# A transformer block with spline-coded feed-forward weights: a third key tile turned by VectorE, x loaded turned, shorter weight sums

## The chip, the core and the metric

The kernel runs on one core of a Trainium2 chip. The metric is the device time of one execution in microseconds: 546.9 us is the median of three runs before the change (546.57 to 549.12). The engines are called PE (TensorE: matrix products and transposes through the identity matrix, with PEld as its loading of weights), DVE or VectorE, ACT or ScalarE, POOL or GpSimd, and SP, whose queue issues nearly all transfers here. Each engine takes its instructions in the order in which they were written; they wait for each other through semaphores.

## The reference

x has 4 batches of 512 tokens with 512 features. The block computes a layer norm without weights and adds two branches that both read its result:

```python
x = x + attention(xn) + ffn(xn)            # xn = (x - mean) / sqrt(var + 1e-5)
# attention: 16 heads of 32, causal
scores = q k^T / sqrt(32) + slope[h] * (key - 511)      # then the causal mask
out = (softmax(scores) @ v) @ Wo + bo
# ffn: each weight matrix (2048 x 512 or 512 x 2048) is a Catmull-Rom
# spline through 8134 control points, read row by row
inter = silu(xn @ gate_w.T) * (xn @ up_w.T)
y = inter @ down_w.T
```

A weight row is a sum of a few control points, each times a known coefficient that depends only on the position. All is in float32.

## The kernel before, in words

**Two stages.** The attention stage takes the four batches one after the other and prepares the feed-forward stage's tables beside it; the feed-forward stage then runs by written plans (line 1273, carried out by `carry_out`). The attention stage ends in the profile at 387.8 us, where the first gate product (line 1135) starts.

**Units.** The attention's work is cut into 64 units, `units` at line 850: batch b, group hg of four heads, tile i of 128 queries. Unit number n is 16 b + 4 hg + i; four units with the same b and hg are called a group here. Unit i looks at the keys of tiles 0 to i. The loop at line 1074 writes one step per unit, and in step n:

- `normalize(units[n-1])`: VectorE's reciprocal of the sums (line 907), then four scalings of p by GpSimd (909);
- `scores(u)`: PE's products for four heads (865; the step i = 0 also makes those of i = 1), then for each head one VectorE instruction that adds the distances and gives the row's minimum, "minima" below (878). The four PSUM banks of the scores are the same in each unit, so the next products wait for these;
- `exponentials(u)`: ScalarE's exp with the minimum as bias and the sum as second result (894);
- `turn(old, c)` for unit n-3: p, with keys along the free axis, must have keys on the partitions for the product with v. Key tiles c = 0 and 2 go through PE, four transposes to a `pT` copy by ScalarE (922, 923);
- `swap(n-2)`: key tiles 1 and 3 go through VectorE instead, which transposes 32x32 blocks (937); four transfers per unit then move the blocks to their partitions (`moved`, 945). For this the keys of the odd tiles are stored in another order (814 to 822), and `dists` holds the distances in that order (589 to 612). `SLOTS` lists the (query tile, key tile) pairs;
- at the end of a group's last step, `values` of the group before (966);
- `items[n]`, `small[n]` and `early[n]`: lists filled from line 988 on with what else belongs to this step: projections q and k of the next group, values of the next batch, the output projection of the batch before, statistics and norms of the next batch.

**Norm and turn of x.** For the next batch, `stat_steps` computes mean and root, `norm` writes xn with tokens on the partitions (767), and `turn_it` turns it through PE, four transposes and a ScalarE copy per token tile (782, 783), into `xnT`. Tiles 0 to 3 are normalized at units 7 to 10 of a batch and turned at 8 to 11.

**The tables of the feed-forward stage.** `row_weight_steps` (616) makes the reduced gate and up weights: eight terms, each a product of 128x1024 (646) and, but for the first, an addition (649), for two halves. `down_steps` (664) makes those of down: 14 terms of 512 or 640 columns (690, 693), five for each of two pieces and four for the third. Each takes coefficients and points that SP loads to the spare space of `feat`. `some_weights` (1068) places them, twice in each step, by a budget of estimated costs. `stretch_moments` (503) multiplies xnT by a basis (510), copies three PSUM banks out and sends them to DRAM; the buffers `out` are two, so the third copy waits for the first's transfer (525, 528). `copy_rows` (543) lets GpSimd issue the copies that gather a batch's table.

Of the kernel before, what the change touches and what calls it, by code (L numbers as in the profile page):

```python
# [12 lines left out]
F32 = mybir.dt.float32  # L13
# [5 lines left out]
P = 128  # L19
# [6 lines left out]
NG = 4  # L26
# [4 lines left out]
SLOTS = [(1, 1), (2, 1), (3, 1), (3, 3)]  # L31
# [17 lines left out]
NCV = 5  # L49
NX = 9 + 4  # L50

COPIES = (1, 1, 4, 1)
NW, NW4 = 11, 4
NST = NW4 + 1

DOWN_STEPS = [("v", lo, hi, c) for lo, hi in ((0, 5), (5, 9)) for c in range(NCV)]
DOWN_STEPS += [("m", 0, NB, c) for c in range(4)]

# [276 lines left out]

def own_points(parts, points):


    values = parts[:, :, :, :9].transpose(0, 4, 3, 1, 2)
    values = values.reshape(P, 9, 2, P // 2, NCD)  # L340
    moments = parts[:, :, :, 9:].transpose(3, 4, 0, 1, 2)
    moments = moments.reshape(P, NB, 2, P // 2, NCD)
    strip = np.broadcast_to(points[:, None, None], (NB, Q32, 9, P, NCD)).reshape(values.shape)
    group = np.broadcast_to(points[None], (P, NB, P, NCD)).reshape(moments.shape)
    own = {}
    for kind, a, number, n in (("v", values, strip, NCV), ("m", moments, group, 4)):
        hit = (a != 0.0).any(axis=3)
        first = np.where(hit.any(axis=3), hit.argmax(axis=3), 0)
        first = np.minimum(first, NCD - n)[:, :, :, None, None] + np.arange(n)
        first = np.broadcast_to(first, (*a.shape[:4], n))  # L350
        few = np.take_along_axis(a, first, axis=4)
        assert np.count_nonzero(few) == np.count_nonzero(a)
        shape = (*a.shape[:2], P, n)
        own[kind] = few.reshape(shape), np.take_along_axis(number, first, axis=4).reshape(shape)
    steps = [[a[:, lo:hi, :, c].reshape(-1) for a in own[k]] for k, lo, hi, c in DOWN_STEPS]
    return *(np.concatenate(a) for a in zip(*steps)),
# [20 lines left out]
_coef = _coef.reshape(NB, NB, P, NCG, 2, Q32).transpose(3, 1, 5, 0, 4, 2)  # L377
COEF = single(_coef.reshape(NCG, P, NB, 2, P))
# [20 lines left out]
def block_kernel(  # L399
    ctx: ExitStack,  # L400
    tc: tile.TileContext,
    xT: bass.AP,
    cols: bass.AP,
# [28 lines left out]
    feat = {0: keep.tile([P, NB, 2, S], F32, name="feat")}  # L432
    table = [dram.tile([P, NB, 2, S], F32, name=f"table{b}") for b in range(B)]
# [10 lines left out]
    edge = [keep.tile([P, S], F32, name=f"edge{k}") for k in range(2)]  # L444
    lone = [keep.tile([P, S], F32, name=f"lone{k}") for k in range(2)]
    basist = keep.tile([P, NRT, ND], F32, name="basist")
# [20 lines left out]
    dists = [wp.tile([P, S], F32, name=f"dist{k}") for k in range(2)]  # L467
# [84 lines left out]
    with ExitStack() as att:  # L552
# [19 lines left out]
        for k in range(2):  # L572
            nc.gpsimd.memset(lone[k], 0.0)
            nc.gpsimd.memset(edge[k], 0.0)
# [9 lines left out]
        nc.sync.dma_start(out=basist, in_=basis)  # L584
# [4 lines left out]
        for k, dist in enumerate(dists):  # L589
            for t in range(NB):  # L590
                part = dist[:, t * P : (t + 1) * P]
                shape, steps = part, [[1, P]]
                if t % 2 == k:
                    shape = part.rearrange("p (r y) -> p r y", y=Q32)
# [4 lines left out]
                    base=1 - S + t * P,  # L599
# [3 lines left out]
                if t == NB - 1:  # L603
# [12 lines left out]
        def row_weight_steps(first_down):  # L616
            size = NB * 2 * P
            shaped = lambda a: a.rearrange("p (q x n) -> p q x n", q=NB, x=2)
            spare = [
                feat[0].rearrange("p c h s -> p (c h s)")[:, k * size : (k + 1) * size]  # L620
                for k in range(4)
            ]
            temps = [wd[:, :size], wd[:, size : 2 * size]]
            tabs, points = {}, {}

            def load(c):
                def go():
# [735 lines left out]
```

## Time and profile before, and how to read it

| what | value |
|---|---|
| median of three runs | 546.9 us |
| the profiled execution's own time | 543.63 us |
| its span, first to last instruction | 541.4 us |
| attention stage's end (first L1135) | 387.8 us |
| PE turns of p, L922 | 384, 56.5 us busy |
| PE turns of x, L782 | 64, 9.5 us busy |
| DVE block transposes, L937 | 64, 43.4 us busy |
| ScalarE copies behind the turns, L923 and L783 | 96 and 16, 54.8 and 9.2 us busy |
| row weights, L646 and L649 | 16 and 14, 1.21 and 1.26 us each |
| down weights, L690 and L693 | 14 and 11, 0.64 to 0.86 and 0.64 to 1.20 us each |

A row such as "L922 PE MATMUL mm<-ident,p 128*128 128x128 f32 x384" names the line, the engine, the operation, what it writes and reads, its shape and its count. A float32 product appears as two records on PE. "DVE inv L907 <- ACT p L894" in the list of waits says that the first waited for the second. Matmul records overlap, since their ends are modelled: the time that PE spends on one is read from the next one's start.

### The profile page before, as it was taken

To read this page: it belongs to the slowest core of one execution; us is meant where nothing else is said; L and a number is where in the kernel's file an instruction comes from. 1 tells how busy PE (TensorE), PEld (TensorE's weight loads), DVE (VectorE), ACT (ScalarE), POOL (GpSimd) and SP (SyncE) were. 2 spreads that over 40 slices of the span, in tenths; PEclk is the share of its full clock that TensorE was granted. 3 is DMA by queue.
4 is the path that set the end of the run, shared out by engine and by line. 5 is a ranking of instruction groups with operands and counts; after the bars stand their busy time and mean duration, and the time that the engine had idled before them with its cause. 6 is when DMAs were issued, how large, how long until landed. Compare 5 with 4: busy or idle time off the path is not lost.

```text
span 541.4 us, 12182 instructions
## 1 busy us (share of the span) xinstructions
PE 530.3 (98%) x4268; PEld 268.0 (50%) x4268; DVE 352.8 (65%) x990; ACT 296.0 (55%) x798; POOL 243.8 (45%) x436
## 2 busy tenths in 40 slices
PE   7999999999999999999999999989999999999997
PEld 6645545444445544444554454545334555747552
DVE  6169978888677877667676456563135584865836
ACT  2466875665466665646757588883313433624222
POOL 3045635574266565446656567671017232332310
PEclk9999999999999999999999999979999999999999
DMA  8933487575545785745743325464656565665344
GB/s 317 321 122 70 114 213 215 160 194 155 161 144 147 243 276 166 214 142 146 215 123 89 92 67 148 137 188 118 174 165 197 184 221 197 199 203 181 119 164 166
DMA packets 63805, 92.98 MB, mean 172 GB/s; under 512 B 10528, under 2 KB 35104, under 8 KB 63232
## 3 DMA queue, kind: packets, MB, share of 16 engines
q1 hardware_dynamic: 59136, 83.79, 51.5%
q0 software_dynamic: 4608, 8.40, 5.3%
q8 instruction: 34, 0.56, 0.4%
q14 instruction: 27, 0.22, 0.1%
HBM read 50.74 MB, written 23.68 MB: 137 GB/s over the span
## 4 chain that ended last, share of the span: by engine, by line
PE 84%; DVE 5%; DMA 5%; ACT 3%; SPq 2%; issue 1%; DVEq 0%; ACTq 0%
PE mm L798 17%; PE g L1135 9%; PE mm L837 9%; PE s L865 7%; PE mm L922 7%; PE mm L482 6%; PE o L1236 6%; PE c L966 5%; PE o L1182 4%; PE o L1253 3%; PE o L482 3%; ACT p L894 2%; DVE p L878 2%; PE s L482 2%; PE mm L510 2%; PE o L1135 2%
## 5 line engine op out<-in xcount | busy, mean ns | idle before, releaser
L909 POOL TENSOR_SCALAR p<-p,inv 128x128 f32<-128x128 f32 (+3 forms) x256 | 147.5, 589 | 172.1 <-DVE inv L907 122.1
L894 ACT ACTIVATE p<-p,low 128x128 f32<-128x128 f32 (+3 forms) x256 | 141.3, 555 | 48.9 <-DVE low L878 48.3
L878 DVE CUSTOM_DVE_ANT_0 p<-s,dist 128x128 f32<-128x128 f32 (+3 forms) x256 | 108.8, 481 | 21.8 <-PE s L865 21.5
L1158 POOL COPY made<-inner 128x512 f32<-128x512 f32 x64 | 38.9, 637 | 104.2 <-DVE inner L1157 81.5
L923 ACT COPY pT<-mm 128x512 f32<-128x512 f32 x96 | 54.8, 577 | 40.3 <-PE mm L922 40.0
L1135 PE MATMUL g<-feat,wT 32*64 32x512 f32 x864 | 65.3, 592 | 0.0
L1150 ACT ACTIVATE act<-g 128x512 f32<-128x512 f32 x64 | 33.0, 602 | 57.0 <-PE g L1135 56.7
L865 PE MATMUL s<-kT,qT 32*128 32x512 f32 (+3 forms) x512 | 57.4, 479 | 2.2 <-DVE low L878 2.0
L798 PE MATMUL mm<-xnT,wk 128*128 128x512 f32 (+1 forms) x136 | 59.3, 579 | 0.2 <-ACT xnT L783 0.2
L837 PE MATMUL mm<-wv,xnT 128*128 128x512 f32 x128 | 58.1, 596 | 1.1 <-ACT xnT L783 1.1
L798 PE MATMUL mm<-xnT,wq 128*128 128x512 f32 (+1 forms) x136 | 57.8, 567 | 0.0
L922 PE MATMUL mm<-ident,p 128*128 128x128 f32 x384 | 56.5, 283 | 0.4 <-ACT pT L923 0.3
L922 PEld LDWEIGHTS mm<-ident,p 128*128 128x128 f32 x384 | 42.5, 142 | 25.6 <-issue 17.1
L894 ACT ACTIVATION_READ_ACCUMULATOR p<-p,low 128x1 f32 x256 | 48.8, 191 | 0.0
L937 DVE STREAM_TRANSPOSE blocks<-p 128x512 f32<-128x512 f32 x64 | 43.4, 696 | 0.0
L1157 DVE TENSOR_TENSOR inner<-g,act 128x512 f32<-128x512 f32 x44 | 27.3, 683 | 21.7 <-PE g L1135 10.7
L1135 PEld LDWEIGHTS g<-feat,wT 32*64 32x64 f32 x864 | 30.6, 131 | 21.3 <-issue 10.6
L865 PEld LDWEIGHTS s<-kT,qT 32*128 32x128 f32 x512 | 24.5, 186 | 32.8 <-issue 16.2
L798 PEld LDWEIGHTS mm<-xnT,wk 128*128 128x128 f32 x136 | 24.5, 189 | 25.1 <-issue 21.5
L546 POOL DMA_DIRECT2D table<-samples x64 | 36.9, 583 | 0.0
L1236 PE MATMUL o<-inner,dRM 32*64 32x512 f32 x512 | 36.6, 588 | 0.0
L798 PEld LDWEIGHTS mm<-xnT,wq 128*128 128x128 f32 x136 | 24.7, 190 | 22.4 <-issue 21.7
(105 smaller groups left out, 656.3 us busy)
## 6 DMA issues: line engine op xcount, KB each, us to landing
moved<-blocks SPq DMA_DIRECT2D x128, 64.0 KB, 2.1
moved<-blocks SPq DMA_DIRECT2D x64, 128.0 KB, 3.0
feat<-table SPq DMA_DIRECT2D x16, 512.0 KB, 4.3
inner<-made SPq DMA_DIRECT2D x32, 256.0 KB, 3.5
table<-samples POOLq DMA_DIRECT2D x64, 88.0 KB, 3.0
xp<-in_xp_dram SPq DMA_DIRECT2D x16, 256.0 KB, 5.1
feat<-in_coef_dram SPq DMA_DIRECT2D x8, 512.0 KB, 8.8
feat<-in_rowpts_dram SPq DMA_DIRECT2D x32, 128.0 KB, 5.1
```

The costliest lines, as they stand in the source:

```text
L482: nc.tensor.matmul(ps, lhsT=wsb["o"][:, c, r * P : (r + 1) * P], rhs=ctxT[b][:, c, :], start=(c == 0), stop=(c == NB - 1),)
L798: nc.tensor.matmul(ps[0][:, tokens], lhsT=wsb[name][:, c, hg * P : (hg + 1) * P], rhs=xnT[b][:, c, tokens], start=(c == 0), stop=(c == NB ...
L837: nc.tensor.matmul(ps[0], lhsT=xnT[b][:, c, t * P : (t + 1) * P], rhs=wsb["v"][:, c, :], start=(c == 0), stop=(c == NB - 1),)
L865: nc.tensor.matmul(banks[b, hg][j][:, at : at + (k + 1) * P], lhsT=qk[b, hg, "q"][rows, k * P : (k + 1) * P], rhs=qk[b, hg, "k"][rows, : ( ...
L878: nc.vector.tensor_tensor_reduce(out=p[:, j, :nk], in0=ps[j], in1=dists[i % 2][:, S - nk :], scale=-SLOPES[hg * NG + j], scalar=BIG, op0=A ...
L894: nc.scalar.activation(p[:, j, :nk], p[:, j, :nk], AF.Exp, bias=low[:, j : j + 1], scale=-1.0, accum_out=total[:, j : j + 1],)
L909: nc.gpsimd.tensor_scalar(p[:, j, :nk], p[:, j, :nk], inv[:, j : j + 1], 1.0, ALU.mult, ALU.mult)
L922: nc.tensor.transpose(ps[:, j, :], p[:, j, c * P : (c + 1) * P], ident)
L923: nc.scalar.copy(pT[b, hg, c][:, :, (i - c) * P : (i - c + 1) * P], ps)
L937: nc.vector.transpose(own[:, :, k].rearrange("p r j k -> p j r k"), soft[u][0][:, :, c * P : (c + 1) * P].rearrange("p j (r k) -> p j r k" ...
L1135: nc.tensor.matmul(ps[k][cols, :], lhsT=wT[rows, q, 2 * w + part, cols], rhs=feat[b][rows, q, part, :], start=(part == 0), stop=(part == 1),)
L1236: nc.tensor.matmul(sums[b][r][cols, :], lhsT=dR[rows, a, cols], rhs=o[rows, :], start=(a == 0), stop=False,)
```

## The change

It does the following, all of it before or in the attention stage but for one step:

- **Key tile 2** is turned by VectorE's block transposes too. PE turns key tile 0 alone (four transposes per unit, one ScalarE copy). `moved` gets seven slots (one unused); units i = 1, 2 and 3 now transpose 1, 2 and 3 blocks of 128x512 instead of 1, 1 and 2. The keys of tiles 1 to 3 all have the other order, with one table of distances of ten 128x128 pieces.
- **x of batches 1 to 3** is loaded already turned from a new input (`xn0`, 1 MB per batch). Mean and root are written to DRAM as rows and read back to all partitions, and `norm_turned` subtracts and multiplies in `xnT` itself, two VectorE instructions per token tile. The statistics stand earlier and have one small instruction less per refinement.
- **Four-term weights.** Each weight keeps only the four points that touch it: row weights have 4 terms of two halves instead of 8, down weights 12 terms instead of 14. The points of the rows come whole from DRAM instead of being broadcast. The terms are placed once per step by a running credit, and their loads are issued one step later.
- **Reciprocals behind minima**: `scores(u)` is written ahead of `normalize(units[n-1])`, and the exponentials are no longer split around the turns.
- **Places**: `stretch_moments` of batches 0 and 2 move from units 20 and 34 to 6 and 42; k of one group a unit later in batches 1 to 3; values of batch 3 from units 42, 43, 46, 47 to 46, 50, 51, 54; the first output projection of batch 2 from unit 63 to 60. `edge` and the down basis are set up by a new step E of the feed-forward plan instead of at the start.

```diff
+        def write_rows(b):
+            of = slice(b * NB, (b + 1) * NB)
+            for k, part in enumerate((mean[:, of, 0], rstd[:, of])):
+                nc.sync.dma_start(out=token[b][k].rearrange("(t p) -> p t", p=P), in_=part)
+
+        def read_rows(b):
+            rows[b] = tp.tile([P, 2, S], F32, name="rows")
+            nc.sync.dma_start(out=rows[b], in_=token[b].partition_broadcast(P))
+
+        def load_turned(b):
+            xnT[b] = xtp.tile([P, NB, S], F32, name="xnT", bufs=2)
+            nc.sync.dma_start(out=xnT[b], in_=xn0[b].rearrange("(c p) s -> p c s", p=P))
+
+        def norm_turned(b, t):
+            at = slice(t * P, (t + 1) * P)
+            for k, op in enumerate((ALU.subtract, ALU.mult)):
+                own = rows[b][:, k, at].unsqueeze(1).to_broadcast([P, NB, P])
+                nc.vector.tensor_tensor(xnT[b][:, :, at], xnT[b][:, :, at], own, op)
...
-        def turn(u, c):
+        def turn(u):
...
+            if i == 0:
+                pT[b, hg] = tp.tile([P, NG, S], F32, name="pT")
...
-                moved[b, hg] = tp.tile([P, NB, len(SLOTS), NG, Q32], F32, name="moved")
+                moved[b, hg] = tp.tile([P, NB, NSLOT, NG, Q32], F32, name="moved")
+            at = slice(2 * i - 2, 3 * i - 2)
+            own = tp.tile([P, NB, i, NG, Q32], F32, name=f"blocks{i % 2}")
+            for c in range(i):
                 nc.vector.transpose(
...
-                project_out(b - 1, [at + n for n in (15, 16, 17, 18)])
+                project_out(b - 1, [at + n for n in (12, 16, 17, 18)])
             if b + 1 < B:
                 for t in range(NB):
-                    go, turn_it = norm(b + 1, t)
-                    small[at + 7 + t].append(go)
-                    items[at + 8 + t].append(turn_it)
-                for n, t in ((10, 0), (11, 1), (14, 2), (15, 3)):
+                    small[at + 8 + t].append(lambda b=b, t=t: norm_turned(b + 1, t))
+                items[at + (4, 5, 4)[b]].append(lambda b=b: load_turned(b + 1))
+                items[at + 5].append(lambda b=b: write_rows(b + 1))
+                items[at + 6].append(lambda b=b: read_rows(b + 1))
+                for t, n in enumerate(((10, 11, 14, 15), (10, 11, 14, 15), (14, 18, 19, 22))[b]):
                     items[at + n].append(value(b + 1, t))
-                for n, step in zip((1, 2, 3, 4, 5, 5, 6, 6, 7), stat_steps(b + 1)):
+                for n, step in zip((1, 1, 2, 2, 3, 3, 3, 4, 4), stat_steps(b + 1)):
                     small[at + n].append(step)
...
-            items[(20, 18, 34, 66)[b]].append(lambda b=b: stretch_moments(b))
+            items[(6, 18, 42, 66)[b]].append(lambda b=b: stretch_moments(b))
...
         for n in range(len(units) + LAG):
...
+            if u:
+                scores(u)
             if 0 <= n - 1 < len(units):
                 normalize(units[n - 1])
-            if u:
-                scores(u)
...
-            budget = 0.0 if n < NB else (1.2, 1.2, 0.6, 1.2)[n % NB] - 0.6 * len(small[n])
-            some_weights(0.5 * budget)
-            for step in items[n]:
+            if n >= NB:
+                credit = min(credit + TERMS[n % NB] - 0.3 * len(small[n]), 1.0)
+            due, late = late, []
+            while done < len(terms) and credit > 0.0:
+                cost, *term = terms[done]
+                if term:
+                    nc.vector.tensor_tensor(*term)
+                done += 1
+                credit -= cost
+                if done in loads:
+                    late.append(loads[done])
+            for step in (*items[n], *small[n], *due):
                 step()
-            for step in small[n]:
-                step()
-            some_weights(0.5 * budget)
             move()
...
-        "G0 P0 U0 F0 P1 G1 P2 U1 F1 X4 P3 G2 V2 F2 X4 G3 V3 F3",
+        "G0 P0 U0 F0 P1 G1 P2 U1 F1 X4 P3 G2 V2 F2 X4 E G3 V3 F3",
```

## The prediction, made before the changed kernel ran

> **What bounds the kernel now.** First the page's busy times:
>
> ```profile
> span 541.4 us, 12182 instructions
> ...
> PE 530.3 (98%) x4268; PEld 268.0 (50%) x4268; DVE 352.8 (65%) x990; ACT 296.0 (55%) x798; POOL 243.8 (45%) x436
> ```
>
> PE is busy 98% of the span, but a record's end is modelled, so I read start times in PE's timeline (start, length, line, count):
>
> ```profile
> 169.85 1.09 PE L922 MATMUL mm<-ident,p 128*128 128x128 f32 x8
> 170.78 0.60 PE L782 MATMUL mm<-ident,xn 128*128 128x128 f32 x4
> 171.21 3.67 PE L837 MATMUL mm<-wv,xnT 128*128 128x512 f32 x8
> ...
> 292.70 1.14 PE L865 MATMUL s<-kT,qT 32*128 32x512 f32 x8
> ...
> 311.42 2.24 PE L865 MATMUL s<-kT,qT 32*128 32x512 f32 x8
> ```
>
> Eight turns hold PE 0.93 us (0.116 each), four turns of x 0.43 (0.109 each), and the next work follows at once: while PE has other work, each turn removed is time removed. The last two rows are the same scores; the first lead on after 1.07 us, the second after 2.17, because their four banks come free one by one behind VectorE's minima. That is a hidden stall, and unit 50 has no projection to cover it. Next the engines by group of four units (start:end, length, then PE, PEld, DVE, ACT, POOL busy, clock); groups count from 0 at 23.9:
>
> ```profile
> 41.40:57.80 16.40, 16.40 (x105) 8.30 (x104) 15.08 (x57) 11.38 (x37) 8.50 (x15) 1.00 0.30 65
> 57.80:82.60 24.80, 24.67 (x141) 12.68 (x140) 19.79 (x59) 19.09 (x54) 11.15 (x18) 1.00 0.72 180
> ...
> 253.90:277.90 24.00, 24.00 (x137) 12.21 (x136) 15.01 (x49) 17.44 (x50) 13.19 (x23) 1.00 0.50 145
> ...
> 333.40:350.00 16.60, 16.60 (x107) 8.52 (x106) 9.28 (x41) 13.48 (x41) 11.54 (x23) 1.00 0.50 136
> 350.00:369.00 19.00, 16.62 (x94) 8.73 (x94) 11.74 (x46) 13.67 (x44) 11.70 (x23) 0.82 0.52 149
> ```
>
> VectorE has room almost everywhere; groups 14 and 15 are bound by no engine. The chain of waits there, and two rows of the list of waits (total, times, longest), say why:
>
> ```profile
> 346.84 1.21 ACT p L894 x4
> 348.05 0.02 issue
> 348.08 0.08 DVE inv L907
> ```
> ```profile
> DVE inv L907 <- ACT p L894: 29.1, 22, 2.5
> DVE out L525 <- DMA moments<-out: 15.2, 4, 4.6
> ```
>
> The reciprocal waits for ScalarE's exponentials, the next unit's minima stand behind it, and the next exponentials behind those. The second row is another stall: each stretch holds VectorE's queue for 3.8 us on average.
>
> **What the change does, step by step.** The profiled execution took 543.63 us around its span of 541.4; the median is 546.9, 3.3 above. I sum against the execution and carry the difference over to the median.
>
> *PE.* Key tile 2 is turned in units 2 and 3 of a group: 8 of 24 turns, 128 in all. In groups 1 to 13 and the tail that saves 14 x 0.93 = 13.0 us; groups 14 and 15 are counted by themselves below. Twelve x tiles of four turns: 12 x 0.43 = 5.2. Together 18.2. Ends: by the mean busy time (56.5/384 = 0.147 each) 5 us more; nothing where PE isn't the bound.
>
> *VectorE.* Added: 32 block transposes (43.4/64 = 0.68) = 21.7 us, 1.36 per group, and 24 subtractions and products of 128x512; the 128x512 additions of L693 take 0.74 and the products of L690 0.67, so 24 x 0.68 = 16.3, less 12 x 0.60 for the old norms. Removed: 8 products and 8 additions of row weights (8 x 1.21 + 8 x 1.26 = 19.8), 2 of each for down (3.1), 12 small ones (2.0). Net +6 us over the attention; the placing matters more. Walking the budgets through both programs, the weights of groups 2, 3 and 4 cost 7.4, 9.9 and 7.4 us before and 3.7, 3.7 and 2.5 after. Group 2 becomes 19.8 - 3.7 + 1.4 + 3.8 (norms) = 21.3, against PE's 24.8 - 0.9 - 1.8 - 0.8 (its late first scores, below) = 21.3: both full. Group 10 becomes 15.0 - 2.2 + 1.4 + 3.8 = 18.0 (its new stretch copies cost what its two fewer value copies give).
>
> *ScalarE and GpSimd.* ScalarE loses 32 + 12 copies of 0.57 (25 us), only of use where PE isn't the bound. GpSimd keeps its normalizing; two more iotas, and the memsets moved, cost under 1 us in a prologue that waits for loads. The normalizing starts behind the minima, up to 2.4 us later (four of 0.61); block transposes follow a unit later and turns two, which hides it.
>
> *Queues.* SP issues as many moves as before (12 a group), with 8.4 MB more; a 128 KB move lands in 3.0 us, a 64 KB one in 2.1, so 192 KB in about 3.9; the values come two units later. Loading x turned (1 MB a batch, as the samples' transfer) has three to four units of lead. Weight loads fall from 40 to 16 for the rows and 28 to 24 for down, moved to a unit later but 4 to 6 terms ahead. Means and roots go out as 1,024 packets of 4 bytes a batch: q1 spent 51.5% of 16 x 541.4 us on 59,136 packets, 75 ns each, so 4.8 us on 16 engines plus 1.8 (the smallest transfer shown), and the broadcast back takes 4.3 to 8.8 (512 KB rows). 10.9 to 15.4 us against three units of 4.1 in group 1: nothing or 3 us late once; I take nothing, since later batches have 20 us.
>
> *Stalls that go.* Values of batch 3 move into units 50, 51 and 54: 1.1 us at unit 51, 1.3 at 55 and 0.6 behind it. Group 14: PE's own rows sum to 2.8 (scores), 4 x 0.49 (turns), 7.1 (q, k), 2.3 (values) = 14.1, ScalarE's to 12.3; I take 14.5 for 16.6. Group 15: PE 10.5 with the output projection that now fills unit 60, ScalarE 12.5, VectorE 13.1; I take 14 for 19. Together 10.1 us. Ends: nothing, if the exponentials still set the pace, or 1 more.
>
> *Stalls that come.* A stretch now stands at units 6 and 42 instead of 20 and 34. VectorE's wait for its transfer stays, and after units 6 and 42 no q projection covers the minima behind it, as one did at 19, 21 and 35. At unit 6 the scores of 8 come 3.3 us late (VectorE free 8.5 us after the stretch starts, first bank 0.8 later, paced 0.6 a head; PE out of work after 8.0), instead of 1.1 + 0.8 late now, and unit 21 is rid of 0.5: +1. Group 2, both engines full: +1. Unit 34 loses its filler: +1.1. Group 10: PE 24.0 - 6.9 + 3.6 - 0.9 - 1.8 = 18.0, VectorE 18.0 + 3.8 of waiting = 21.8: +3.8. Unit 48, no value ahead: +0.8. Together 7.7; ends: nothing, and twice that.
>
> *After 387.8* nothing changes but a 512 KB load and two memsets at step E, three PE steps (5.7 us) ahead of the first use: 4.3 to 8.8 us to land, so 0 to 3; I take 0.
>
> Sum: -18.2 - 10.1 + 7.7 = -20.6. Span 520.8, execution 523.0, median **526.3 us**.
>
> **Weighed against the Trainium skill.** The clock was 0.50 from 357 to 363 us, after a longest empty stretch of 1.96 us with PE busy 1.42 of 3 us. The page "TensorE: Matmul & The Clock Gate" (section "What's actually happening") halves the clock only after an idle window of 3.4 us: no new stall here is that long, and the sum would stay. By the row a sparse stretch is enough: two more dips of 3 us, -14.6. I keep the row's price for the upper end. The page "VectorE: DVE Perf Modes" (section "The three transpose paths") calls a plain DMA that transposes by strides 19 times slower: speaking against the rows' write-out, an estimate of 19 x 1.8 = 34 us for each. No run here shows it yet.
>
> **Rivals.** *VectorE takes over* (0.24): stalls that come double (+7.7), two clock dips (+6): gain 6.9, 540 (532 to 544). For: groups 1, 2 and 10 near full. Against: row weights halved. *Everything pays* (0.15): no new stall, 518.6, with 0.147 a turn 514. *Nothing left* (0.05): the exponentials pace batch 3 and VectorE the rest: 544.2 to 549.6. *Slower* (0.06): the means' packets run on four of 16 engines: 19.2 + 1.8 + 8.8 = 30 us, and the norms at units 8, 24 and 40 block VectorE in front of the minima for 18, 7 and 10 us: 526.3 + 35 = 561. It ends above 546.9 from a landing of about 25 us on. Speaking against: 128 partitions would have to miss the spread that 75 ns a packet rests on.
>
> **How the numbers follow.** Forecast 0.50 (520 to 531). Left out of 514 to 540: nothing left 0.05, slower 0.06, the upper part of VectorE's case 0.05, 0.02 below. A measurement can tell 0.5% (2.7 us) from no change: faster = 0.50 + 0.23 + 0.15 = 0.88, same 0.06, slower 0.06.
>
> **What would show it.** Turns down to 256 (and 16 for x), PE's attention end near 367 instead of 387.8; groups 14 and 15 near 14 us; the reciprocals' wait for ScalarE mostly gone; PE waiting after units 7 and 43. Wrong, if norms wait on the rows' DMA, if PE shows gaps in groups 1 to 13 beyond 8 us, or if the stage after attention grows.

## The result, and the profile after

The changed kernel takes 577.99 us (median of 4 runs, 575.05 to 579.47) beside 547.19 for the kernel before on the same chip (4 runs, 546.57 to 549.12): 1.055 times as long, with a 95% interval of 1.0496 to 1.0604. The forecast was 526.3, its range 514 to 540, with 0.06 on "slower". Both sign and size were wrong.

The page of the profile after, its first lines and the chain:

```profile
span 577.7 us, 11735 instructions
## 1 busy us (share of the span) xinstructions
PE 528.2 (91%) x4092; PEld 255.1 (44%) x4092; DVE 364.5 (63%) x1002; ACT 275.1 (48%) x754; POOL 249.7 (43%) x440
...
PE 68%; DMA 14%; DVE 9%; SPq 4%; issue 3%; ACT 1%; POOL 0%; DVEq 0%; POOLq 0%; ACTq 0%
```

PE fell from 98% of the span to 91%, and transfers are 14% of the chain where they were 5%. PE's busy time hardly fell (530.3 to 528.2) although 176 turns are gone, because part of its work ran at half clock (0.944 granted on average, 0.993 before) and lasted twice as long. The stretches after by the table of windows (start:end, length, PE, PEld, DVE, ACT, POOL busy, then PE's clock, DMA share and GB/s): groups 1, 2, 10, 14 and 15, those shown of before.

```profile
41.50:72.60 31.10, 20.79 (x113) 9.27 (x112) 17.48 (x56) 10.56 (x35) 9.23 (x16) 0.84 0.60 153
72.60:97.10 24.50, 24.11 (x112) 10.95 (x112) 21.77 (x60) 17.14 (x50) 14.06 (x20) 0.93 0.80 244
275.70:296.20 20.50, 18.55 (x114) 8.15 (x113) 15.65 (x46) 10.69 (x34) 11.41 (x18) 0.96 0.62 163
361.80:377.70 15.90, 15.81 (x97) 7.56 (x96) 11.30 (x43) 13.61 (x43) 11.97 (x23) 1.00 0.66 175
377.70:396.60 18.90, 16.68 (x88) 8.35 (x88) 11.64 (x43) 12.06 (x38) 13.37 (x26) 0.73 0.67 189
```

Group 1 is the loudest: 31.1 us where it was 16.4, with PE idle for 10. Two rows of the list of waits are the answer to those shown of before, two are new:

```profile
PE c L948 <- DMA moved<-blocks: 13.9, 2, 7.2
DVE out L527 <- DMA moments<-out: 13.8, 4, 4.5
PE c L948 <- DMA rows<-token: 10.1, 1, 10.1
DVE inv L890 <- ACT p L877: 4.3, 2, 3.8
```

The reciprocals no longer wait for the exponentials (4.3 us for 29.1), as forecast. The values (L948) now wait 24 us for transfers; before, PE idled 0.7 us in all ahead of the moved values. (The third row names the rows, but the values read the moved blocks: by the trace's completion events the last of these landed at 68.3 and the rows at 69.5, after PE had restarted.) Line numbers here and in the lines below are those of each run's own kernel: scores 847, values 948, turns 905, block transposes 918, moves 928 in the changed one.

**The hole in group 1.** PE's timeline and SP's, in the same time:

```profile
57.39 1.06 PE L948 MATMUL c<-pT,v 128*32 128x512 f32 x8
68.51 2.79 PE L948 MATMUL c<-moved,v 128*32 128x384 f32 x24 [10.06 <-DMA rows<-token]
```
```profile
49.47 0.60 SPq L754 DMA_DIRECT2D token<-mean  x1
50.17 0.78 SPq L754 DMA_DIRECT2D token<-rstd  x1
51.00 0.54 SPq L627 DMA_DIRECT2D feat<-in_coef_dram  x1
51.58 0.43 SPq L628 DMA_DIRECT2D feat<-in_rowpts_dram  x1
53.15 2.83 SPq L928 DMA_DIRECT2D moved<-blocks  x4
60.28 0.33 SPq L758 DMA_DIRECT2D rows<-token  x1
```

SP writes means and roots out at 49.47 and 50.17, 1,024 packets of 4 bytes. Then 1 MB of weights' tables, then the moves that the values need, and only at 60.28 the read of the rows, which had to wait for the writes to land: by the completion events the last did at 60.26, 10.8 us after the first was issued (14.7 us in groups 5 and 9). What the transfer engines did meanwhile (same columns as above):

```profile
48.00:51.00 3.00, 3.00 (x10) 1.38 (x9) 2.83 (x14) 0.69 (x3) 1.48 (x2) 1.00 0.97 316
51.00:54.00 3.00, 3.00 (x17) 1.45 (x16) 3.00 (x7) 2.58 (x9) 1.42 (x4) 1.00 0.26 24
54.00:57.00 3.00, 3.00 (x20) 0.89 (x16) 2.23 (x10) 2.19 (x7) 0.60 (x2) 1.00 0.33 37
57.00:60.00 3.00, 1.45 (x16) 0.16 (x8) 0.00 (x0) 0.78 (x3) 1.25 (x3) 1.00 0.60 33
60.00:63.00 3.00, 0.00 (x0) 0.00 (x0) 0.00 (x0) 0.00 (x0) 0.00 (x0) 0.89 0.62 107
63.00:66.00 3.00, 0.00 (x0) 0.00 (x0) 0.00 (x0) 0.00 (x0) 0.00 (x0) 0.50 1.03 392
```

From 51 to 60 they carry 24 to 37 GB/s, though a megabyte waits behind; at 63 that comes through at 392. Tables and moves stand behind the small packets. The trace's packet records show more of how: the 4-byte packets have all started by 52.2 and take 9 ns each, 0.6 us if spread over 16 engines. But of the 4,096-byte packets behind them only 72 start from 54 to 62, at 0.91 us each on average, and in the next two microseconds 149, at 0.16 each. So it isn't the small packets' own time on the engines: what follows crawls until they have landed. Why, no run here shows. Meanwhile PE's clock falls to 0.50, and what follows the hole runs at half speed: 24 products in 2.79 us (1.48 undisturbed). The same hole opens at 167 (6.70 us) and 265 (7.17), in groups 5 and 9.

**The hole behind the attention.** PE's timeline at step E, then SP's:

```profile
444.23 2.30 PE L1113 MATMUL g<-feat,wT 32*64 32x512 f32 x26
453.89 5.82 PE L1168 MATMUL o<-inner,basist 32*64 32x512 f32 x64 [7.37 <-issue]
```
```profile
446.29 0.60 SPq L551 DMA_DIRECT2D feat<-table  x1
446.93 0.46 SPq L1128 DMA_DIRECT2D basist<-in_basis_dram  x1
```

PE is through with its work at 446.5, and only at 446.93 does SP issue the load of `basist`. Written three PE steps ahead, it stands in SP's queue behind transfers that wait for later work of other engines. First gate to last product took 148.8 us before, 158.0 after.

### The profile page after: what moved, and what is told of

It reads as the page before. It is cut to its first block, busy times and chain, and to the rows that moved or that the text cites. A ratio compares the mean times of both kernels' runs of the same rounds, so it can differ in the third digit from the quotient of the medians.

```text
span 577.7 us, 11735 instructions
## 1 busy us (share of the span) xinstructions
PE 528.2 (91%) x4092; PEld 255.1 (44%) x4092; DVE 364.5 (63%) x1002; ACT 275.1 (48%) x754; POOL 249.7 (43%) x440
## 4 chain that ended last, share of the span: by engine, by line
PE 68%; DMA 14%; DVE 9%; SPq 4%; issue 3%; ACT 1%; POOL 0%; DVEq 0%; POOLq 0%; ACTq 0%
PE mm L781 16%; PE mm L819 9%; PE g L1113 8%; PE s L847 6%; PE c L948 5%; PE mm L905 5%; PE o L1168 4%; PE o L1222 4%; DMA moved<-blocks 4%; PE mm L484 3%; DVE p L861 3%; DMA feat<-in_rowpts_dram 3%; PE o L484 3%; DMA mid<-xt 2%; DMA moments<-out 2%
## 5 line engine op out<-in xcount | busy, mean ns | idle before, releaser
L892 POOL TENSOR_SCALAR p<-p,inv 128x128 f32<-128x128 f32 (+3 forms) x256 | 152.4, 608 | 194.1 <-DVE inv L890 172.1
L918 DVE STREAM_TRANSPOSE blocks<-p 128x512 f32<-128x512 f32 x96 | 61.5, 678 | 18.2 <-DMA moved<-blocks 14.8
L847 PE MATMUL s<-kT,qT 32*128 32x512 f32 (+3 forms) x512 | 62.2, 490 | 6.9 <-DVE low L861 5.9
L1113 PE MATMUL g<-feat,wT 32*64 32x512 f32 x864 | 63.7, 592 | 0.0
L781 PE MATMUL mm<-xnT,wq 128*128 128x512 f32 (+1 forms) x136 | 61.7, 599 | 1.5 <-ACT pT L906 1.5
L906 ACT COPY pT<-mm 128x512 f32<-128x512 f32 x64 | 36.7, 580 | 37.2 <-PE mm L905 37.2
L948 PE MATMUL c<-moved,v 128*32 128x384 f32 (+2 forms) x384 | 29.0, 443 | 25.3 <-DMA moved<-blocks 13.9
L1143 DVE TENSOR_TENSOR inner<-g,act 128x512 f32<-128x512 f32 x44 | 27.3, 684 | 32.5 <-PE g L1113 26.5
L847 PEld LDWEIGHTS s<-kT,qT 32*128 32x128 f32 x512 | 28.0, 194 | 40.6 <-issue 15.4
L905 PE MATMUL mm<-ident,p 128*128 128x128 f32 x256 | 43.1, 295 | 0.0
L905 PEld LDWEIGHTS mm<-ident,p 128*128 128x128 f32 x256 | 29.8, 147 | 26.7 <-issue 19.1
L1113 PEld LDWEIGHTS g<-feat,wT 32*64 32x64 f32 x864 | 29.5, 131 | 22.2 <-issue 11.7
```

The lines of the kernel that those rows point to most:

```text
L781: nc.tensor.matmul(ps[0][:, tokens], lhsT=wsb[name][:, c, hg * P : (hg + 1) * P], rhs=xnT[b][:, c, tokens], start=(c == 0), stop=(c == NB ...
L847: nc.tensor.matmul(banks[b, hg][j][:, at : at + (k + 1) * P], lhsT=qk[b, hg, "q"][rows, k * P : (k + 1) * P], rhs=qk[b, hg, "k"][rows, : ( ...
L892: nc.gpsimd.tensor_scalar(p[:, j, :nk], p[:, j, :nk], inv[:, j : j + 1], 1.0, ALU.mult, ALU.mult)
L905: nc.tensor.transpose(ps[:, j, :], p[:, j, :P], ident)
L918: nc.vector.transpose(own[:, :, c].rearrange("p r j k -> p j r k"), soft[u][0][:, :, (c + 1) * P : (c + 2) * P].rearrange("p j (r k) -> p ...
L948: nc.tensor.matmul(ps[j * HD : (j + 1) * HD, c * P :], lhsT=vals[b][:, c, hg * P + j * HD : hg * P + (j + 1) * HD], rhs=part(j), start=(c ...
```

## The experiments

The runs stand on several chips, each beside runs of the kernel before; between chips I compare ratios (0.01 is about 5.45 us), within one the medians. Theory W: the rows' write-out holds up all transfers. E: the late `basist`. V: VectorE has no room for what it was given. Group lengths in the profiles, from the first scores of a group to those of the next (us; "FFN" is first gate to the start of the last row of products). The runs are called e1 to e20 in the text. A profile is one execution: those of e15 and e3 are the slowest of their kernels (544.2 and 554.2 beside medians of 539.2 and 551.3), so a difference of a microsecond in one group says little.

| kernel | 1 | 2 | 4 | 5 | 8 | 9 | 10 | 11 | 12 | 13 | 14 | 15 and tail | FFN |
|---|---|---|---|---|---|---|---|---|---|---|---|---|---|
| before | 16.4 | 24.8 | 22.8 | 31.1 | 22.3 | 26.2 | 24.0 | 22.2 | 19.8 | 13.4 | 16.6 | 37.9 | 148.8 |
| after | 31.1 | 24.5 | 21.2 | 37.6 | 20.4 | 33.8 | 20.5 | 22.6 | 24.5 | 18.5 | 15.9 | 36.7 | 158.0 |
| e1_packed | 26.9 | 24.5 | 21.2 | 26.3 | 20.6 | 26.0 | 19.8 | 21.9 | 24.5 | 18.5 | 16.1 | 38.1 | 156.4 |
| e6_tile2 | 20.3 | 23.8 | 24.9 | 33.2 | 26.6 | 24.7 | 23.0 | 21.0 | 19.2 | 19.1 | 16.7 | 37.6 | 148.9 |
| e8_old_early_stretch | 22.8 | 23.0 | 21.2 | 33.2 | 21.2 | 26.4 | 17.4 | 18.6 | 24.5 | 18.5 | 15.9 | 36.4 | 149.7 |
| e12_no_tile2 | 19.5 | 24.0 | 22.3 | 31.4 | 22.3 | 27.0 | 17.7 | 20.0 | 25.6 | 16.7 | 16.4 | 34.0 | 148.3 |
| e16_terms_late_k | 20.3 | 23.4 | 21.2 | 30.0 | 21.2 | 25.5 | 17.6 | 18.6 | 24.5 | 15.1 | 15.7 | 35.4 | 149.7 |
| e19_best_no_tile2 | 16.8 | 24.0 | 22.3 | 30.5 | 22.3 | 26.5 | 17.7 | 20.0 | 25.6 | 15.1 | 16.4 | 33.8 | 149.2 |

### Rows and step E

**Packed rows (e1).** VectorE turns the eight columns of means and roots by its 32x32 transpose, and four transfers write them as 32 packets of 128 bytes.

```diff
-                nc.sync.dma_start(out=token[b][k].rearrange("(t p) -> p t", p=P), in_=part)
+                nc.vector.tensor_copy(pack[:, k * NB : (k + 1) * NB], part)
+            nc.vector.transpose(out=packT, in_=pack)
+            for k in range(NB):
+                nc.sync.dma_start(
+                    out=token[b].rearrange("k (t r y) -> r (k t) y", r=NB, y=Q32)[k],
+                    in_=packT[k * Q32 : k * Q32 + 2 * NB],
+                )
```

> Edit: means and roots leave for DRAM in 32 packets of 128 bytes per batch instead of 1,024 of 4 bytes; VectorE first turns a 128x32 tile by its block transpose (three small instructions per batch). All else is as in the changed kernel. Theory W (the 4-byte packets hold up every transfer behind them on SP's queue, and the values then wait for the moved blocks): the three holes of PE at 57 to 68, 166 to 174 and 264 to 272 us go (10.1 + 6.9 + 7.4 us) and with them the half clock behind each (some 4 us each), so about 36 us less than the changed kernel's 578: 538 to 546. Rival V (VectorE's added work and the added 13 MB of transfers make the loss, the holes are only where it shows): within 8 us of the changed kernel, 570 to 578.

559.85 us, ratio 1.0291 (1.0249 to 1.0333): in between. The holes of groups 5 and 9 are gone (37.6 to 26.3, 33.8 to 26.0), so W holds for them, and the ratio falls by 0.026, some 14 us. In group 1 the packed writes land 1.2 us after their issue, and the 187 packets of 4,096 bytes that start from 57 to 60 take 0.21 us each on average. But group 1 stays long:

```profile
64.51 2.79 PE L957 MATMUL c<-moved,v 128*32 128x384 f32 x24 [5.60 <-DMA rows<-token]
```

There SP issues the writes at 54.88, the tables (1 MB) behind them, the moves from 57.11 and the rows' broadcast (512 KB) at 61.44, all inside one short group. VectorE had the last unit's blocks ready at 53.3 (the moves left at 53.15 in the changed kernel), but the writes stand ahead of the moves in SP's order and wait for VectorE's packing, which ends at 54.85: the moves leave almost 4 us later than they could.

**Step E first (e2).**

```diff
-        "G0 P0 U0 F0 P1 G1 P2 U1 F1 X4 P3 G2 V2 F2 X4 E G3 V3 F3",
+        "E G0 P0 U0 F0 P1 G1 P2 U1 F1 X4 P3 G2 V2 F2 X4 G3 V3 F3",
```

> Edit: step E of the feed-forward plan (basis load and two memsets) comes first in the plan instead of ahead of G3. The hole of PE between 446.6 and 453.9 us is then no longer a wait for the basis: theory E says 7.4 us of waiting and some 2 us of half clock go, 567 to 570. The rival, that PE waits there for something else (GpSimd's copies or the rows of inner), leaves 575 to 578.

565.93 us, ratio 1.0394 (1.0364 to 1.0424), 0.016 less than after; the last stage is back at 148.8 us. E is shown: 8.5 us by the ratios, 9.2 by the stage. (The expectations below that say "12.0" took medians of two chips.)

**x turned on PE (e3).** Four-byte writes, rows, the load of x turned and its normalizing all go; the old norm and the four turns of each token tile come back.

```diff
-                    small[at + 8 + t].append(lambda b=b, t=t: norm_turned(b + 1, t))
-                items[at + (4, 5, 4)[b]].append(lambda b=b: load_turned(b + 1))
-                items[at + 5].append(lambda b=b: write_rows(b + 1))
-                items[at + 6].append(lambda b=b: read_rows(b + 1))
+                    go, turn_it = norm(b + 1, t)
+                    small[at + 7 + t].append(go)
+                    items[at + 8 + t].append(turn_it)
```

> Edit: x of batches 1 to 3 is normalized and turned on PE at the old places (units 7 to 10 and 8 to 11 of a batch), nothing is loaded turned, no rows are written or read; all else as in the changed kernel. Theory W: the three holes go as in the packed variant, PE takes 5.2 us more for the turns of x, VectorE 9 us less: 540 to 550. Rival V: VectorE's part falls too, so this alone does not part W from V; it does together with the packed variant (V: this one falls by 15 us or more, the packed one by less than 8).

551.28 us, ratio 1.0123 (1.0087 to 1.0158), with the late `basist` still in it (last stage 159.2 us). Loading x turned, meant to save 5.2 us of turns, cost 0.043 of the ratio: 23 us, 14 of them in the packets and 9 in the rest of it (the load, the broadcast, VectorE's normalizing), which this run doesn't part. V alone is out: it had packed rows gain less than 8 us.

**The writes on another queue (e5).** They leave SP's queue for ScalarE's.

```diff
-                nc.sync.dma_start(out=token[b][k].rearrange("(t p) -> p t", p=P), in_=part)
+                nc.scalar.dma_start(out=token[b][k].rearrange("(t p) -> p t", p=P), in_=part)
```

> Edit: the two 4-byte write-outs per batch are issued from ScalarE's queue instead of SP's; all else as in the changed kernel. If the packets only stand in the way of what follows on the same queue (W, queue), the moved blocks and the weights no longer wait behind them and most of the holes goes: 540 to 555; the rows still land some 9 us after the start of the write. If the packets hold the 16 engines themselves whatever the queue (W, engines), the holes stay: 570 to 580. Two issues of 0.5 us on ScalarE per batch cost nothing that PE waits for.

582.75 us, ratio 1.0692 (1.0649 to 1.0735). The three holes ahead of values stay, in its timeline:

```profile
63.21 2.79 PE L948 MATMUL c<-moved,v 128*32 128x384 f32 x24 [4.35 <-DMA moved<-blocks]
...
173.27 2.79 PE L948 MATMUL c<-moved,v 128*32 128x384 f32 x24 [7.44 <-DMA mid<-xt]
...
277.26 2.79 PE L948 MATMUL c<-moved,v 128*32 128x384 f32 x24 [13.41 <-DMA moved<-blocks]
```

The writes land 9.8 to 20.9 us after their issue there. So it isn't their place in SP's order: the packets hold up what all queues share. The Trainium skill says as much on its page "DMA: Bandwidth & Descriptors" (section "Issuing engines are not separate DMA queues"): starting transfers from several engines saves only the time to start them. This run agrees: the holes stayed, and the ratio rose by 0.014.

**Packed rows and E first (e4).**

> The packed rows and step E first together. Theory "two separate losses": the write-out costs the attention and the late basis costs the stage after it, and they add: 559.9 us with packed rows alone less the 12.0 us that E first took from the changed kernel, 546 to 550, about the kernel before, with group 5 and 9 below 27 us, group 1 still near 27, and 149 us behind the attention. Rival "one loss": basis only came late because the queue lagged behind the write-outs, which packed rows already mend in part: 553 or more.

549.92 us, ratio 1.0085 (1.0062 to 1.0108); last stage 148.5, group 1 26.9. Against packed rows alone 0.021 (11 us), where E alone gave 0.016: within the spread the two losses are separate and add. Without them the change is still no gain, so the terms that should have brought 28 us don't either.

### Tile 2, reciprocals, stretches

**Tile 2 alone (e6).** Before, with the new `dist`, `turn`, `swap`, k layout and values, and `basist` and `edge` set up at the head of the last stage.

```diff
-SLOTS = [(1, 1), (2, 1), (3, 1), (3, 3)]
+NSLOT = 7
...
+            if old:
+                turn(old)
             if u and not keep_it:
-                exponentials(u, range(2))
-            for c in turns[1:]:
-                turn(old, c)
-            if u and not keep_it:
-                exponentials(u, range(2, NG))
+                exponentials(u, range(NG))
```

> The kernel before with key tile 2 turned by VectorE and moved, and nothing else of the change but that basis and edges are set up at the head of the feed-forward stage (for space). Theory "PE is the bound": 128 turns of 0.116 us less, all in groups whose next work follows at once: 10 to 14 us below before (530 to 534 where before takes 544), turns 256, groups 1 to 13 each about 0.9 shorter. Rival "VectorE and the moves pay": 1.36 us more of block transposes in a group and the values waiting for moved blocks give half of it back or more: less than 6 us gained.

554.22 us, ratio 1.0166 (1.0103 to 1.0229): 9 us slower. "PE is the bound" falls. Where nothing is late the groups shrink (2, 9 to 12: 0.6 to 1.5 us each); groups 1, 4, 5, 8 and 13 grow by 2 to 6. PE's timeline in group 13, and the group of values' products in the table of groups (busy, mean, then idle ahead of it and for what), in e6 and then in the kernel before:

```profile
333.71 2.55 PE L859 MATMUL s<-kT,qT 32*128 32x512 f32 x8 [0.83 <-DVE low L873]
336.20 1.66 PE L960 MATMUL c<-pT,v 128*32 128x512 f32 x8
341.38 2.79 PE L960 MATMUL c<-moved,v 128*32 128x384 f32 x24 [3.52 <-DMA moved<-blocks]
```
```profile
L960 PE MATMUL c<-moved,v 128*32 128x384 f32 (+2 forms) x384 | 26.8, 416 | 11.6 <-DMA moved<-blocks 5.8 <-DMA moments<-out 3.9 <-DMA feat<-in_downtab_dram 1.4
L966 PE MATMUL c<-moved,v 128*32 128x384 f32 (+1 forms) x256 | 19.8, 380 | 0.7 <-DMA feat<-in_downtab_dram 0.4 <-issue 0.2
```

The last unit's three block transposes end at 333.1, SP issues their 192 KB until 336.2, PE asks at 337.9, and they land at 341.3. Half clock surrounds the hole (it began at 336.5).

**Reciprocals behind minima alone (e7).**

```diff
-            if 0 <= n - 1 < len(units):
-                normalize(units[n - 1])
             if u:
                 scores(u)
+            if 0 <= n - 1 < len(units):
+                normalize(units[n - 1])
```

> The kernel before with the two calls in the loop in the other order, so that a unit's minima stand ahead of the reciprocal of the unit before; nothing else. Theory "stalls that go": the reciprocal's wait for the exponentials (29.1 us in 22 waits) goes, the groups 14 and 15 become 1 to 3 us shorter each and the rest stays: 2 to 5 us below before. Rival "late scaling": GpSimd's scaling and so the turns and values start up to 2.4 us later, and PE waits for them in groups that have little other work: not faster, or slower by 1 to 5 us.

542.15 us, ratio 0.9949 (0.9921 to 0.9977): 2.9 us faster; the wait drops to 2.9 us. Groups 14 and 15 hardly move (16.6 to 16.4, the tail 37.9 to 36.8): the wait was mostly harmless there too.

**x on PE, E first, stretches back (e8).**

```diff
-            items[(6, 18, 42, 66)[b]].append(lambda b=b: stretch_moments(b))
+            items[(20, 18, 34, 66)[b]].append(lambda b=b: stretch_moments(b))
```

> The changed kernel with x turned on PE as before (no rows), basis and edges set up first, and the stretches back at units 20, 18, 34 and 66. From the run with x turned on PE (551.3) less 12.0 for E it would be 539.3. Theory "the stretches' places cost": group 1, group 2 and group 10 lose what the moved stretches put there, 3 to 6 us more gained: 533 to 536. Rival "fillers": the long groups 2, 11 and 13 come from the k projections a unit later and from the terms' placing: 538 to 541, with groups 2, 11 and 13 as they were (28.0, 23.6, 16.8).

541.78 us, ratio 0.9938 (0.9905 to 0.9972). From e3 that is 0.0185, E by itself is 0.016 to 0.021: the stretches' places are worth nothing that shows here. Group 2 loses 5 us and group 5 takes 6: a stretch costs where it stands. Of the groups that "fillers" held to stay as they were, 13 stayed long (18.5), but 2 and 11 fell to 23.0 and 18.6, so neither theory holds as it was put.

**The last unit's transposes one step earlier**, with tile 2 (e10), in before as control (e11), and on e8 (e13). In e10 and e11 the normalized x also lies in another pool, for space.

```diff
-            move = lambda: None
-            if 0 <= n - LAG_SWAP < len(units):
-                move = swap(units[n - LAG_SWAP])
+            moves = []
+            for lag in (LAG_SWAP, 1):
+                if 0 <= n - lag < len(units) and (units[n - lag][2] == NB - 1) == (lag == 1):
+                    moves.append(swap(units[n - lag]))
```

> Key tile 2 alone, as in the run that took 554.2, but VectorE turns a group's last unit (three block transposes, 192 KB to move) one step earlier, behind those of the third unit; the values stay where they are. Theory "moves come late": tile 2 lost because the last unit's moved blocks land after PE has asked for them (idle 3.5, 3.9 and 2.2 us ahead of values, and half clock behind); with a step more in hand the holes ahead of the values go and the removed turns show: 531 to 538. Rival "VectorE full": 1.36 us a group too much on VectorE, whose minima come late; the place of the transposes changes little: 550 to 556.

> Control: the kernel before with only the same shift, the last unit's two block transposes a step earlier. In before PE idles 0.7 us in all ahead of values on moved blocks, so by "moves come late" nothing changes: 543 to 546. If the shift by itself moves the time by over 3 us either way, the run with tile 2 and the shift can't be read as mending lateness alone.

> The run of 541.8 with the last unit's block transposes a step earlier. PE idles only 1.2 us ahead of values there, and its long groups 1, 5, 12 and 13 start behind scores that wait for minima. Theory "moves come late" as the whole of tile 2's price: no hole to mend, 539 to 542. Rival "they fill other gaps": the transposes leave the step in which the next scores' minima are due, and groups 12 and 13 (24.5 and 18.5) shorten too: 533 to 538.

551.53 (ratio 1.0116, 1.005 to 1.0181), 554.35 (1.0158, 1.0092 to 1.0223) and 563.79 (1.0337, 1.0275 to 1.0399). The control fell: the shift alone costs 10 us, since VectorE now waits for GpSimd's scaling (block transposes 22.4 us in e11, 30.4 in e13) with the minima behind it. So e10, though inside the range of "VectorE full", can't be read against before, and e13 misses both of its theories by over 20 us. Against e11 e10 can be read: with the shift in both, tile 2 is no longer 9 us slower but 2.8 faster (intervals overlap), and PE idles 0.8 us ahead of the moved values instead of 11.6. That speaks for late moves as tile 2's price there, but VectorE's new waits in both kernels could hide part of that price; and the earlier place is no cure.

**e8 without tile 2 (e12).** The exponentials are split around the turns again, too.

```diff
-NSLOT = 7
+SLOTS = [(1, 1), (2, 1), (3, 1), (3, 3)]
```

> The run of 541.8 (x turned on PE, E first, stretches back; four-term weights, reciprocals behind minima and the moved values kept) with key tile 2 back on PE. Theory "PE is the bound": 128 turns return, 8 to 13 us slower: 550 to 555. Rival "tile 2 costs, the rest gains": what tile 2 alone did to before (+9.2) goes: 530 to 536, below both kernels.

542.42 us, ratio 0.9967 (0.9934 to 1.0): the same as e8, neither theory. By groups both are at work: with tile 2 eleven are shorter by 0.3 to 1.4 us (10.2 in all), and 1, 5, 13 and the tail longer by 9.3.

### Where VectorE is full, and the fillers

In e8's group 1 (42 to 62 us, the columns of the windows) VectorE is busy 19.1 of 20 us:

```profile
42.00:62.00 20.00, 17.61 (x74) 8.23 (x77) 19.08 (x64) 13.05 (x42) 10.75 (x18) 0.83 0.63 168
```

e15 starts the weights at unit 8; e16, e17 and e18 then put back k, the values of batch 3, and both.

```diff
-            if n >= NB:
+            if n >= 2 * NB:
...
-                items[at + 4 * hg + 1 + (b > 0 and hg == 1)].append(project("k", nb, nh))
+                items[at + 4 * hg + 1].append(project("k", nb, nh))
...
-                for t, n in enumerate(((10, 11, 14, 15), (10, 11, 14, 15), (14, 18, 19, 22))[b]):
+                for t, n in enumerate(((10, 11, 14, 15), (10, 11, 14, 15), (10, 11, 14, 15))[b]):
```

> The run of 541.8 (x turned on PE, E first, stretches back) with the weights' terms beginning at unit 8 instead of unit 4; nothing left out. Theory "VectorE full": in group 1 VectorE has work without a gap from 42 to 62 us, so three products of 1.2 us less, and the half clock behind the late scores, take group 1 from 22.8 to 17 to 19: 536 to 539. Rival "late moves": group 1 is long because the values wait for moved blocks: its length stays above 21 and the time within 540 to 543.

> As e15, and the k projections of every second group back one unit earlier. Theory "fillers": unit 53 gets its filler back and group 13 goes from 18.5 to below 15, while nothing else changes: 3 to 4 us below e15. Rival "no matter": the work only changes place inside groups 12 and 13, within 1 us of e15.

> As e15, and the values of batch 3 back at units 42, 43, 46 and 47. By my sum their later places gave 3.0 us (units 51 and 55): 3 us above e15, group 10 back to 24, 12 to 20, 14 and 15 unchanged. Rival "only moved": PE was never out of work at those units for long, the four products of 3.6 us change groups and the time stays within 1 us of e15.

> Both back. If placements only add, e16's and e17's differences from e15 sum. Rival: with values and k at their old places group 13 is the 13.4 us of before and the pair gives more than the sum, 533 to 536.

Medians beside 545.34 for before: e15 539.17 (ratio 0.9899, 0.9832 to 0.9967), **e16 533.37 (0.9778, 0.9739 to 0.9816)**, e17 540.05 (0.9898, 0.9845 to 0.9951), e18 539.41 (0.9856, 0.9806 to 0.9906). e15 is inconclusive: group 1 only falls to 20.9, between the theories; in e16, which has the same group, VectorE isn't full any more and the values wait 2.27 us for moves instead. k in its old place gives 5.8 us, from the unit that got its filler back: group 13 goes from 18.5 to 15.1 and group 5 from 32.8 (in e15) to 30.0, while group 9, the third with a moved k, stays at 25.5. The values in their later places give 6.0 us once k is back (e18 to e16) and nothing while it isn't (e17 to e15, 0.9, inside the spread): the moved k projections take it back. So the places don't add, as e18's first theory had it, and its rival (533 to 536) fails too: with both at their old places group 13 takes 16.2, not the 13.4 of before. e16 beats both kernels.

**What the two PE terms are worth there.** e19 is e16 without tile 2; e20 is e16 with x loaded turned and packed rows.

> The run of 533.4 (x turned on PE, E first, stretches and k projections at their old places, weights from unit 8) with key tile 2 back on PE. Theory "PE is the bound where VectorE has room": eleven groups 0.6 to 1.4 us longer each (10 us in all), group 1, 5, 13 and the tail 3 to 5 us shorter: 538 to 541. Rival "tile 2 gives nothing", as between the runs of 541.8 and 542.4: 532 to 535.

> The run of 533.4 with x loaded turned and normalized by rows, as in the change, but means and roots written in packets of 128 bytes. By my sum the twelve turns of x give 5.2 us: 527 to 530. Theory "the rows' transfers stand ahead of the moves": packed rows lost 8.6 us against x turned on PE (559.9 and 551.3), most of it in group 1, where the load of x (1 MB) and the broadcast (512 KB) share the queue with the moves: 537 to 543.

Beside 546.2 for before: e19 537.76 (ratio 0.9856, 0.9811 to 0.9901), e20 543.87 (0.9938, 0.991 to 0.9967). By ratios tile 2 gives 4.3 us there, good to some 3, in the groups that were to give it; groups 1 and 2 with it (e16) and without (e19):

```profile
41.60:62.00 20.40, 17.29 (x101) 8.45 (x100) 16.05 (x59) 13.19 (x42) 10.51 (x20) 0.94 0.35 78
62.00:85.40 23.40, 23.40 (x131) 11.70 (x130) 16.74 (x49) 15.93 (x47) 10.19 (x16) 0.98 0.76 223
```
```profile
41.80:58.50 16.70, 16.55 (x105) 8.31 (x104) 15.28 (x57) 13.18 (x43) 9.56 (x19) 1.00 0.29 64
58.50:82.50 24.00, 24.00 (x137) 12.22 (x136) 15.56 (x47) 17.62 (x50) 12.18 (x18) 1.00 0.66 204
```

Group 2, where PE is never idle, is 0.6 shorter with it; group 1 is 3.5 longer, with PE idle for 3. e20 lies above both of its ranges: loading x turned costs 8.7 us even with packed rows, mostly in groups 1 and 5 (23.2 and 33.7) and the tail (37.7).

## Why the prediction was wrong, step by step

Forecast and result differ by 50.6 us (-20.6 by the sum, +30.0 by the ratio). By differences of ratios, each good to some 3 us, they lie so: the loaded x 28 (-5.2 forecast, +23.3 measured), step E with the stretches' places about 10 (from e3 to e8), tile 2 about 11 (-13.0, and -1.6 from e12 to e8), the stalls that go with the rest of the scheduling about 8 (-10.1, and -1.8 from before to e12), and the stalls that come about 8 the other way. Two of the signs that the prediction named for being wrong came: gaps of PE beyond 8 us in groups 1 to 13, and a longer stage after the attention.

- **Failed first and most: "Queues"**, the words "nothing or 3 us late once; I take nothing, since later batches have 20 us". I followed the rows to their own reader, the norms, which indeed never waited. I didn't ask what stands behind the packets: tables and moves for units 7, 23 and 39. The trip itself was too short as well: 10.9 to 15.4 us were forecast from the write to the rows' return, and it took 20.1, 19.6 and 20.2 (the write-out 10.8, 14.7 and 14.7 of it, for 6.6). The mean of 75 ns a packet didn't carry over: the small packets themselves take 9 ns, and their landing is what lasts. But even so the norms didn't wait; the price was PE's 24 us of holes and the half clock around them. What failed most was taking a transfer's time as its own affair.
- **Failed: "192 KB in about 3.9; the values come two units later".** Landing was right (3.9 in e8, 4.0 in e6). But the two units of slack are eaten by VectorE's queue, SP's four issues and shared engines: in e6's group 13 4.8 us were left between the last transpose and the request, 8.2 were needed.
- **Failed: step E, "0 to 3; I take 0"**. Lead was counted in PE's steps; the load was issued in SP's order, level with PE's request. 9.2 us.
- **Right in the rows, lost in the sum: 0.93 a group for tile 2.** Eleven groups show 0.3 to 1.4. What failed is "14 x": groups 1, 5, 13 and the tail are not bound by PE once VectorE has the blocks.
- **Mis-sized: "Stalls that go", 10.1.** Reciprocals were worth 2.9 by themselves. The later values are worth 6.0, but only with k in its old place: my list gave the moved k no row at all, and it takes all of that back.
- **"Stalls that come", 7.7**: the lost filler that counted was not the stretch's but k's. The stretches' move costs nothing that the spread lets one see.
- **Group lengths**: 10 was forecast at 21.8 from VectorE's side and took 20.5; 14 took 15.9 (14.5); 15 took 18.9 (14), at a clock of 0.73. 2 took 24.5 (21.3), with VectorE busy 21.8 and PE's clock at 0.93.
- **The rival "Slower"** had the right origin, the small packets, and the wrong place: no norm blocked VectorE. A trip of 20 us, below the 25 that it needed, did more harm than it forecast.
- **The two rules.** For the rows' write-out the page "VectorE: DVE Perf Modes" (section "The three transpose paths") led to an estimate of 34 us each; both together landed after 10.8 to 14.7 here. The page's factor of 19 is against the DMA transpose through the crossbar, and I had put it on the smallest plain transfer: the size is my misuse, not the page's. Of the two prices for the clock, the row's was the one to keep: it fell to 0.50 in e6 at about 336.5, before that kernel's hole of 3.5 us opened at 337.9, when the longest empty stretch in PE's records of the last 5 us was 0.83 and the scores behind it were spread over 2.55 us.

Not settled: why group 1 with tile 2 stays near 20 us after the weights have left it (e15, e16); late moves are seen there, but no run removed them without moving something else. Whether the 4-byte writes would be harmless behind the moves instead of ahead of them was not tried. What the four-term weights give by themselves was not run either: e12, which has them, the reciprocals and the new places, lies 1.8 us below before.

## What to carry to other kernels

A transfer's price is what stands behind it on the shared engines, not when its own reader needs it: list for each added transfer what is issued in the next ten microseconds and who waits for that. Count lead in the order of the engine that issues, not of the one that uses. A turn taken off PE pays in groups where PE is the bound and its substitute lands in time, so multiply by those groups alone, and give every moved instruction a row, the fillers first.

## What the runs showed of the hardware

- 1,024 packets of 4 bytes from SBUF to DRAM landed 10.8 to 14.7 us after the first issue, though each takes 9 ns. In group 1 all 16 transfer engines together carried 24 to 37 GB/s meanwhile, at a DMA share of 0.26 to 0.60, and packets of 4,096 bytes took 0.91 us instead of 0.16; a queue of its own left the holes. As 32 packets of 128 bytes they landed in 1.2 us in group 1 and cost 14 us less over three batches.
- At the hole in group 1 PE's clock was 0.50 from 62.3 us to 72.6, 4.0 us beyond the restart. Short stalls do it too: e8's group 1 had one of 1.97 us, within which the clock fell (at 55.3); its mean was 0.83 over that group's 20 us and 0.51 over the next 3.6.
- VectorE's block transposes of 128x512 take 0.68 to 0.70 us on average in every run, as was forecast (0.68): the price of one wasn't what the sum for tile 2 had wrong.
